# A kernel of four graph-attention layers: score rows spread by DMA through DRAM in place of transposes on TensorE

## Chip, cores and metric

The kernel runs on one core of a Trainium2 chip. The metric is the device time of one execution in microseconds. The engines are named as in the profile: PE (TensorE, with its weight loads PEld), DVE (VectorE), ACT (ScalarE), POOL (GpSimd) and SP (SyncE, which here issues every DMA).

## What is computed

The input is a batch of 128 graphs, each with 128 nodes of 512 features, and an adjacency matrix of 128 x 128 for each. Four layers follow one another. Each takes `h = relu(layernorm(x))` and adds a graph attention over `h` to `x`:

```
layer 0:  scores = leaky(f1[i] + f2[j]), one head, f = h @ (W^T a);  x += elu(softmax(masked scores) @ h)
layer 1:  xl = h @ W1 (4 heads of 256); softmax over the source nodes;  y = elu(att @ xl + b1)
          then xl2 = y @ W2 (one head of 512), attention again;         x += att2 @ xl2 + b2
layer 2:  scores from two dot products of h, one head;                  x += att @ h
layer 3:  xp = h @ W_proj (8 heads of 64); attention;                   x += relu(att @ xp)
```

In every layer a score is the sum of a number of the row's node and a number of the column's node, with a leaky relu of slope 0.2, a mask from the adjacency matrix and a softmax. All data are float32.

## The kernel before

One graph fills the 128 partitions, so a tile is one graph's `x` (128 x 512). Weights are loaded once and prepared in a setup part: the products that give scores are put as extra columns ahead of the weights (`w1x`, `w2x`, `wpx`), so that a projection yields the scores too. A graph is a Python generator, `graph`, which runs `layer0` to `layer3` and yields between stages. A loop lets up to `FLYING` = 7 graphs fly at a time. In each turn it advances each of them by one stage, oldest first, and every `APART` = 11 turns it starts another. So the instructions are written down in an interleaved order, and a planner of the framework then places them on the engines, by that order and by when their inputs are ready, and puts in the semaphores. Each engine works through its own list in order.

The names that matter below:

- `norm_relu` (L178): bn_stats and bn_aggr on DVE (L180, L182), `ve` and `rstd` on POOL (L185, L187), `nmr` on DVE (L190), and `h` on ACT (L192). `h` has three buffers (pool `mid`).
- `dot` (L199): one product of `h` with a vector, on DVE; its results lie in the tile `f0`.
- `transposed` (L217, L219): transposes on PE into a PSUM bank, copied out by ACT.
- `projected` (L284, L293): matmuls with `w1x`, `w2x` or `wpx` on PE, copied to `xl`, `x2` or `x3` by ACT. The first columns of these tiles are the scores.
- `attention`: for each head, a column of scores (one number for each partition) must become a row that stands on all partitions. PE does it with a transpose of the column broadcast over 128 columns (L233). DVE adds the mask and takes the maximum (L240), adds the row's own score (L252 to L259), applies the leaky relu (L262); ACT takes exp with its sum (L266); DVE takes the reciprocal (L275).
- `applied` (L299): the attention matrix is transposed and multiplied with the values.
- layer 1: attention is scaled (L330) and applied (L337), the bias added (L345), and the elu made of L355 (DVE), L357 (exp on ACT) and L359 (DVE), which writes the tile `y` that the matmuls with `w2x` read.
- layer 0 ends with L314 to L319, layer 2 with L378, layer 3 with L393 (PE), L402 and L408 (DVE).
- `loaded` (L415, L419) issues the loads on SP two graphs ahead; the store of a finished graph is L439.

The step that the change replaces is this one:

```
nc.tensor.transpose(
    pb[:, j * P : (j + 1) * P],
    other[:, g + j : g + j + 1].to_broadcast([P, P]),
    ident,
)
```

It is done 15 times for each graph: once in layer 0, four times and once more in layer 1, once in layer 2 and eight times in layer 3.

Of the kernel before, what the change touches and what calls it, by code (L numbers as in the profile page):

```python
# [8 lines left out]
F32 = mybir.dt.float32  # L9
I32 = mybir.dt.int32  # L10
AF = mybir.ActivationFunctionType
ALU = mybir.AluOpType
# [7 lines left out]
FLYING = 7  # L20
# [5 lines left out]
def kernel(  # L26
# [35 lines left out]
    adjp = ctx.enter_context(tc.tile_pool(name="adjp", bufs=3))  # L62
    xpool = ctx.enter_context(tc.tile_pool(name="xpool", bufs=FLYING + AHEAD))
    masks = ctx.enter_context(tc.tile_pool(name="masks", bufs=FLYING))
    big = ctx.enter_context(tc.tile_pool(name="big", bufs=2))
    mid = ctx.enter_context(tc.tile_pool(name="mid", bufs=3))
    small = ctx.enter_context(tc.tile_pool(name="small", bufs=8))
    ps = ctx.enter_context(tc.tile_pool(name="ps", bufs=8, space=PSUM))

    def bank(name):  # L70
        return ps.tile([P, 512], F32, tag="bank", name=name)
# [100 lines left out]


# [49 lines left out]
    def attention(own, other, mask, nh, tag):  # L223
# [4 lines left out]
        for g in range(0, nh, 4):  # L228
            m = min(4, nh - g)
            pb = bank("pb")  # L230
            for j in range(m):

                nc.tensor.transpose(  # L233
                    pb[:, j * P : (j + 1) * P],
                    other[:, g + j : g + j + 1].to_broadcast([P, P]),
                    ident,
                )
            yield
            for j in range(m):
                nc.vector.tensor_tensor_reduce(  # L240
                    out=e[:, g + j, :],
                    in0=pb[:, j * P : (j + 1) * P],
                    in1=mask,
                    scale=1.0,
                    scalar=LOWEST,
                    op0=ALU.add,
                    op1=ALU.max,
                    accum_out=mx[:, g + j : g + j + 1],
                )
# [28 lines left out]
    def projected(lhs, n_k, w, parts, to):  # L278

        width = w.shape[2] // parts  # L280
        for lo in range(0, w.shape[2], width):
            pm = bank("pm")
            for c in range(n_k):
                nc.tensor.matmul(  # L284
                    pm[:, :width],
                    lhsT=lhs[:, c, :],
                    rhs=w[:, c, lo : lo + width],
                    start=(c == 0),
                    stop=(c == n_k - 1),
                )  # L290
                if c % 4 == 3:
                    yield
            nc.scalar.copy(to[:, lo : lo + width], pm[:, :width])  # L293

# [9 lines left out]
    def layer0(xt, mask):  # L304
# [4 lines left out]
        yield  # L309
        e, rz = yield from attention(f[:, 0:1], f[:, 1:2], mask, 1, "e0")  # L310
# [11 lines left out]
    def layer1(xt, mask):  # L322
# [4 lines left out]
        yield from projected(ht, KC, w1x, 3, fx)  # L327
        xl = fx[:, E1:]
        e, rz = yield from attention(fx[:, H1:E1], fx[:, :H1], mask, H1, "e1")
# [32 lines left out]
        yield from projected(y, FC, w2x, 2, gx)  # L362
        yield
        e, rz = yield from attention(gx[:, 1:2], gx[:, 0:1], mask, 1, "e0")
# [3 lines left out]
    def layer2(xt, mask):  # L368
# [4 lines left out]
        yield  # L373
        fb = small.tile([P, 1], F32, tag="fb", name="fb")
        nc.gpsimd.tensor_tensor(fb, f[:, 0:1], b_l2, ALU.add)
        e, rz = yield from attention(fb, f[:, 1:2], mask, 1, "e0")
# [3 lines left out]
    def layer3(xt, mask):  # L380
# [3 lines left out]
        yield from projected(ht, KC, wpx, 2, fx)  # L384
        f, xh = fx[:, :E3], fx[:, E3:]
        yield
        fb = small.tile([P, H3], F32, tag="fb3", name="fb3")
        nc.gpsimd.tensor_tensor(fb, f[:, :H3], b_l3, ALU.add)
        e, rz = yield from attention(fb, f[:, H3:], mask, H3, "e3")
# [32 lines left out]
    def graph(b, xt, a):  # L422
        m0 = masks.tile([P, P], F32, tag="m0", name="m0")
# [6 lines left out]
        yield from layer0(xt, m0)  # L430
# [5 lines left out]
        yield from layer1(xt, m1)  # L436
        yield from layer2(xt, m2)
        yield from layer3(xt, m3)
# [63 lines left out]
```

## Time and profile before

| what | value |
|---|---|
| time, median of 3 runs | 3705.97 us (3705.27 to 3707.51) |
| the profiled execution's own time | 3706.62 us |
| its span, first to last instruction | 3704.8 us |
| PE busy | 3606.2 us, 97% |
| DVE busy | 3075.8 us, 83% |
| ACT busy | 2131.2 us, 58% |
| DMA, mean | 24 GB/s |
| PE clock granted, mean | 0.987 |
| score transposes on PE (L233) | 1920 |

Busy time is the time in which an engine had an instruction in it. Matmuls overlap one another on PE, so a matmul's duration is longer than the time for which it keeps the next one from starting; the distance from start to start is what it costs in a full stretch. The same holds to a lesser degree on DVE and ACT.

### The profile page before, as it was taken

The numbers are of one execution on the slowest core, as the hardware profiler recorded it, in microseconds if no ns is written. First come the engines' busy times: TensorE is split into PE (matmuls) and PEld (weight loads), VectorE is DVE, ScalarE is ACT, GpSimd is POOL, SyncE is SP. The second block draws the span as 40 slices with busy tenths as digits, with TensorE's granted clock in tenths as the row PEclk, the third lists the DMA queues.
The fourth block names the chain that finished last, engine by engine and source line by source line (L and its number), as shares of the span: only waits on it lengthen the run. The fifth ranks groups of instructions, "written<-read, shape, count | busy, mean of one in ns | idle before, by whom it ended". The sixth has DMA issues, their size and how long they took to land.

```text
span 3704.8 us, 60130 instructions
## 1 busy us (share of the span) xinstructions
PE 3606.2 (97%) x19088; PEld 2870.7 (77%) x19088; DVE 3075.8 (83%) x11634; ACT 2131.2 (58%) x6531; POOL 982.2 (27%) x1671
## 2 busy tenths in 40 slices
PE   2999999999999999999999999999999999999997
PEld 1787787788788788788788788788788788778785
DVE  5788888888888888888888888888888888888884
ACT  1455655665565565565665665565565565565563
POOL 1222222222222222222222222232232222222220
PEclk7999999999999999999999999999999999999997
DMA  4000000000000000000000000000000000000000
GB/s 136 4 21 24 21 24 24 21 21 24 21 21 27 21 18 27 21 21 26 21 18 26 21 21 27 21 18 27 21 21 27 20 19 26 21 18 23 16 9 15
DMA packets 60238, 88.54 MB, mean 24 GB/s; under 512 B 7185, under 2 KB 23569, under 8 KB 59921
## 3 DMA queue, kind: packets, MB, share of 16 engines
q1 hardware_dynamic: 59920, 84.70, 6.9%
q8 instruction: 151, 2.47, 0.3%
q14 instruction: 167, 1.36, 0.1%
HBM read 51.13 MB, written 33.55 MB: 23 GB/s over the span
## 4 chain that ended last, share of the span: by engine, by line
PE 96%; DVE 2%; DMA 1%; ACT 1%; POOL 0%; issue 0%; SPq 0%; DVEq 0%; ACTq 0%; POOLq 0%
PE pm L284 60%; PE pt L217 9%; PE pa L299 9%; PE po L337 6%; PE pa L393 6%; PE pb L233 6%; DMA wpx<-in_L_gnn_W_proj_dram 0%; PE ptm L433 0%; ACT e L266 0%; DVE junk L134 0%; DVE st L180 0%; DVE junk L148 0%; DVE e L240 0%; DVE e L262 0%; DVE e L259 0%
## 5 line engine op out<-in xcount | busy, mean ns | idle before, releaser
L266 ACT ACTIVATE e<-e,nm 128x128 f32<-128x128 f32 x1920 | 750.0, 392 | 500.8 <-DVE e L262 494.1
L284 PE MATMUL pm<-w2x,y 128*128 128x257 f32 x4096 | 980.5, 382 | 0.0
L284 PE MATMUL pm<-w1x,ht 128*128 128x344 f32 x3072 | 953.8, 453 | 0.5 <-ACT ht L219 0.5
L284 PEld LDWEIGHTS pm<-w2x,y 128*128 128x128 f32 x4096 | 737.4, 190 | 85.5 <-issue 0.2
L284 PEld LDWEIGHTS pm<-w1x,ht 128*128 128x128 f32 x3072 | 565.1, 191 | 292.7 <-issue 63.1
L319 POOL TENSOR_TENSOR xt<-xt,t 128x512 f32<-128x512 f32 x128 | 163.7, 1279 | 1610.6 <-DVE mv L182 1535.7
L192 ACT ACTIVATE h<-xt,nmr,rstd 128x512 f32<-128x512 f32 x512 | 401.5, 807 | 198.9 <-DVE nmr L190 195.3
L284 PE MATMUL pm<-wpx,ht 128*128 128x264 f32 x2048 | 495.0, 388 | 0.0
L240 DVE CUSTOM_DVE_ANT_0 e<-pb,m 128x128 f32<-128x128 f32 x1920 | 461.6, 280 | 18.2 <-PE pb L233 17.9
L284 PEld LDWEIGHTS pm<-wpx,ht 128*128 128x128 f32 x2048 | 371.9, 192 | 61.9 <-issue 0.2
L217 PE MATMUL pt<-ident,e 128*128 128x128 f32 x1920 | 342.5, 276 | 31.9 <-ACT e L266 21.1
L219 ACT COPY et<-pt 128x128 f32<-128x128 f32 (+1 forms) x768 | 323.4, 421 | 73.3 <-PE pt L217 64.9
L266 ACT ACTIVATION_READ_ACCUMULATOR e<-e,nm 128x1 f32 x1920 | 358.5, 187 | 0.0
L187 POOL TENSOR_TENSOR rstd<-ve,minus_half 128x1 f32<-128x1 f32 x512 | 343.9, 672 | 42.6
L262 DVE SCALAR_TENSOR_TENSOR e<-e 128x128 f32<-128x128 f32 (+2 forms) x640 | 353.8, 553 | 0.0
L180 DVE BATCH_NORM_STATS2 st<-xt 128x6 f32<-128x512 f32 x512 | 342.5, 669 | 3.9 <-POOL xt L319 3.9
L293 ACT COPY x<-pm 128x257 f32<-128x257 f32 (+1 forms) x512 | 184.5, 360 | 269.5 <-PE pm L284 269.2
L293 ACT COPY xl<-pm 128x344 f32<-128x344 f32 x384 | 165.8, 432 | 273.6 <-PE pm L284 273.4
L217 PEld LDWEIGHTS pt<-ident,e 128*128 128x128 f32 x1920 | 243.4, 141 | 68.2 <-ACT e L266 29.2
L359 DVE SCALAR_TENSOR_TENSOR y<-t,y 128x1024 f32<-128x1024 f32 x128 | 156.8, 1225 | 141.3 <-ACT t L357 141.3
L337 PE MATMUL po<-et,xl 128*128 128x128 f32 x2048 | 272.2, 276 | 1.3 <-ACT et L219 1.3
L337 PEld LDWEIGHTS po<-et,xl 128*128 128x128 f32 x2048 | 250.2, 193 | 12.8 <-ACT et L219 2.2
(74 smaller groups left out, 5264.6 us busy)
## 6 DMA issues: line engine op xcount, KB each, us to landing
xt<-in_x_dram SPq DMA_DIRECT2D x128, 256.0 KB, 2.6
out_dram<-xt SPq DMA_DIRECT2D x128, 256.0 KB, 2.0
at<-in_adj_dram SPq DMA_DIRECT2D x32, 256.0 KB, 2.8
w1x<-in_L_gnn_W_dram SPq DMA_DIRECT2D x1, 2048.0 KB, 8.2
w2x<-in_L_gnn_W_dram SPq DMA_DIRECT2D x1, 2048.0 KB, 13.9
wpx<-in_L_gnn_W_proj_dram SPq DMA_DIRECT2D x1, 1024.0 KB, 16.1
w<-in_L_gnn_W_dram SPq DMA_DIRECT2D x1, 1024.0 KB, 9.6
ab<-in_L_gnn_att_src_dram SPq DMA_DIRECT2D x1, 512.0 KB, 4.9
```

What stands on the lines that cost most here:

```text
L180: nc.vector.bn_stats(st6, xt)
L187: nc.gpsimd.tensor_tensor(rstd, ve, minus_half, ALU.pow)
L192: nc.scalar.activation(h, xt, AF.Relu, bias=nmr, scale=rstd)
L217: nc.tensor.transpose(pt[:, j * P : (j + 1) * P], t[:, g + j, :], ident)
L219: nc.scalar.copy(r[:, g : g + m, :].rearrange("p m q -> p (m q)"), pt[:, : m * P])
L240: nc.vector.tensor_tensor_reduce(out=e[:, g + j, :], in0=pb[:, j * P : (j + 1) * P], in1=mask, scale=1.0, scalar=LOWEST, op0=ALU.add, op1= ...
L262: nc.vector.scalar_tensor_tensor(ef, ef, SLOPE, ef, ALU.mult, ALU.max)
L266: nc.scalar.activation(e[:, j, :], e[:, j, :], AF.Exp, bias=nm[:, j : j + 1], accum_out=z[:, j : j + 1],)
L284: nc.tensor.matmul(pm[:, :width], lhsT=lhs[:, c, :], rhs=w[:, c, lo : lo + width], start=(c == 0), stop=(c == n_k - 1),)
L293: nc.scalar.copy(to[:, lo : lo + width], pm[:, :width])
L299: nc.tensor.matmul(pa, lhsT=et[:, 0, :], rhs=values, start=True, stop=True)
L337: nc.tensor.matmul(po[:, (c - g) * P : (c - g + 1) * P], lhsT=xl[:, c * P : (c + 1) * P], rhs=et[:, c * P // F1, :], start=True, stop=True,)
```

## The change

The score rows of most graphs no longer come from PE. `write_rows` issues a DMA on SP which writes the score columns of a tile (1, 4 or 8 for each partition) into a DRAM tile as rows. `read_rows` issues a second DMA, which reads these rows back and spreads them over all 128 partitions of an SBUF tile. `Spread` holds the two together: the read is written down `WRITTEN` = 5 turns after the write, and the first use `READ` = 3 turns after the read. In a projection the write is put right behind the first part, which holds the scores, and the turns of the other parts count. In the first and last `NEAR` = 4 graphs the rows still come from transposes (`far` is false), so that 120 of 128 graphs use the DMAs. `FLYING` goes from 7 to 10, with more buffers for `x` and the masks; the pools are made after the setup part, and a pool `rows` with two buffers for each size and a DRAM pool with four are added.

```diff
-FLYING = 7
+FLYING = 10
+WRITTEN, READ = 5, 3
+NEAR = 4
...
+    dram = ctx.enter_context(tc.tile_pool(name="dram", bufs=4, space=bass.MemoryType.DRAM))
...
+    rows = ctx.enter_context(tc.tile_pool(name="rows", bufs=2))
...
+    def write_rows(cols, n):
+        r = dram.tile([n, P], F32, tag=f"r{n}", name="r")
+        with nc.allow_non_contiguous_dma(reason="a column of scores becomes a row"):
+            nc.sync.dma_start(out=r.rearrange("h p -> p h"), in_=cols)
+        return r
+
+    def read_rows(r, n):
+        t = rows.tile([P, n, P], F32, tag=f"rb{n}", name="rb")
+        nc.sync.dma_start(
+            out=t.rearrange("p h q -> p (h q)"),
+            in_=r.rearrange("h q -> (h q)").partition_broadcast(P),
+        )
+        return [t[:, j, :] for j in range(n)]
+
+    class Spread:
+        def __init__(self, cols, n, far):
+            self.cols, self.n, self.far = cols, n, far
+            self.turns = 0
+            self.r = write_rows(cols, n) if far else None
+
+        def turn(self):
+            self.turns += 1
+            if self.far and self.turns == WRITTEN:
+                self.rows = read_rows(self.r, self.n)
+
+        def rest(self):
+            if self.far:
+                while self.turns < WRITTEN + READ:
+                    yield
+                    self.turn()
+                return self.rows
...
-    def attention(own, other, mask, nh, tag):
+    def attention(own, rb, mask, nh, tag):
...
-                nc.tensor.transpose(
-                    pb[:, j * P : (j + 1) * P],
-                    other[:, g + j : g + j + 1].to_broadcast([P, P]),
-                    ident,
-                )
-            yield
...
+        for j in range(nh):
+            nc.vector.tensor_tensor_reduce(
+                out=e[:, j, :],
+                in0=rb[j],
...
-    def projected(lhs, n_k, w, parts, to):
+    def projected(lhs, n_k, w, parts, to, cols, far):
...
                 if c % 4 == 3:
                     yield
+                    if sp:
+                        sp.turn()
             nc.scalar.copy(to[:, lo : lo + width], pm[:, :width])
+            if lo == 0:
+                sp = Spread(cols, cols.shape[1], far)
+        yield
+        sp.turn()
+        return (yield from sp.rest())
...
     def graph(b, xt, a):
+        far = NEAR <= b < B - NEAR
```

In the texts below x2, x3 and xl are the score columns of the projections with `w2x`, `wpx` and `w1x`, and f0 and f2 those of the dots in layers 0 and 2.

## The prediction

> **What bounds the kernel now.** I read the busy shares first, then a steady stretch, then the chain of waits.
>
> ```profile
> PE 3606.2 (97%) x19088; PEld 2870.7 (77%) x19088; DVE 3075.8 (83%) x11634; ACT 2131.2 (58%) x6531; POOL 982.2 (27%) x1671
> ```
> ```profile
> 1800.00:2100.00 300.00, 300.00 (x1608) 239.91 (x1607) 255.10 (x967) 177.57 (x544) 80.33 (x136) 1.00 0.07 23
> ```
> ```profile
> PE 96%; DVE 2%; DMA 1%; ACT 1%; POOL 0%; issue 0%; SPq 0%; DVEq 0%; ACTq 0%; POOLq 0%
> ```
>
> In 300 us of steady running PE (second number) is never idle, at full clock (1.00); the chain that ended last runs through PE. The timeline of PE gives the price of each piece by its starts:
>
> ```profile
> 1800.25 0.60 PE L217 MATMUL pt<-ident,h 128*128 128x128 f32 x4
> ...
> 1806.38 0.27 PE L233 MATMUL pb<-ident,f 128*128 128x128 f32 x1
> 1806.49 1.95 PE L284 MATMUL pm<-wpx,ht 128*128 128x264 f32 x8
> ...
> 1828.11 0.60 PE L217 MATMUL pt<-ident,h 128*128 128x128 f32 x4
> ```
>
> The same transposes return after 1828.11 - 1800.25 = 27.86 us: one graph. A score transpose (L233) lasts 0.27 but holds PE 0.11. Times below are such start-to-start spacings.
>
> **What the Trainium skill says.** "DMA: Bandwidth & Descriptors", Two DMAs through the same engine are not ordered: a DMA that reads what another wrote must wait, on its issuing engine, for the writer's semaphore. The trace agrees: each x load waits behind the store of its buffer.
>
> ```profile
> 1835.00 0.34 SPq L439 DMA_DIRECT2D out_dram<-xt  x1
> 1837.07 0.33 SPq L419 DMA_DIRECT2D xt<-in_x_dram  x1
> ```
>
> The same page, Rules for kernel authors: a non-contiguous last dimension becomes one descriptor per element. No steady DMA here is of that kind. "TensorE: Matmul & The Clock Gate", Part 1: after some 3.4 us idle PE's clock falls to half. The trace shows a low clock (0.60) where PE is busy 19 of 50 us:
>
> ```profile
> 50.00:100.00 50.00, 18.85 (x56) 11.78 (x57) 31.12 (x111) 12.23 (x29) 15.17 (x23) 0.60 0.02 5
> ```
>
> **What is removed.** 15 score transposes for each of 120 graphs: 15 x 0.11 = 1.63 us, so PE needs 27.86 - 1.63 = 26.2 us a graph. If PE stayed full that would be all: -196 us.
>
> **What is added.** Per graph five writes and five reads on SP, at 0.34 us of issue (rows above): 3.4 us, with 0.96 MB read. As bandwidth that is nothing (the DMA share is 0.07). What counts is the order. The planner, which places every instruction as soon as its inputs are ready, does not keep the five and three turns. In the built order of the instructions SP's period is: x2 write, f0 write, their reads, xl write, x3 write, their reads, f2 write, its read, store, load. Each pair of reads stands right behind its writes, so SP waits there for the landing, with all later writes queued behind it; the x load queued last is not missed, since it comes two graphs (55 us) ahead of its use. DVE uses the rows at once as well: `e0` on x2's row directly follows the dots that give f0, and the eight `e3` on x3's row directly follow `e1`. While DVE waits there, these are queued behind: the end of layer 0, layer 2's dots, `y` of layer 1 and the end of layer 3. This order repeats exactly for 112 of 128 graphs. So that the spread does not keep the distance that the code asks for is no rival but my starting point.
>
> **The loop that this closes** runs from the end of the elu's `y` instruction (L359), which PE's w2x matmuls await, to the end of the next graph's. Every engine works in order, so each step below waits for the one above. Lines are those of before; spacings are from the DVE, ACT, PE and POOL timelines of before.
> - DVE to h: variance to `nmr` through POOL took 1829.47 to 1830.96, 1.49; twice, with `nmr` 0.08 and L330 0.61 between: 3.67. Then small ones and masks of layer 2's e0: 0.75. Its leaky relu to the ACT start 0.32, exp 0.40. ACT has that exp ahead of layer 3's h (0.81): 5.95, say 6.0.
> - PE behind that h: five transposes 0.55, one w2x matmul 0.435, a transpose 0.11, four w2x 1.74, four w1x 2.32, four transposes 0.44, four wpx 1.78: 7.37.
> - ACT copies x3: 0.27 until it starts, 0.36: 14.0 in all.
> - SP writes x3's 8 columns (w), then reads them as rows (r).
> - DVE: seven `e3` 1.47, L316 0.33, `e3` 0.21, L317 0.65, two dots 1.22, bn_stats delayed by POOL's add of t0 to 4.72; neg, add, small ones, relu to 7.2; two L345, L402, L408 to 10.2; L355, mask, xt, small ones, bn_stats 2.3, which cover ACT's exp; L359 1.15: 13.65.
>
> Sum: 14.0 + 13.65 = 27.65 + w + r. Without any DMA time it is already the present period.
>
> **The unknown DMA times.** w: not below the store's landing, 2.0. x3 is 1024 elements of 4 bytes, 64 per DMA engine; queue q1's packets took on average 6.9% of 16 x 3704.8 / 59,920 = 68 ns, 4.4 us for 64. Doubling it for a partial write gives at most 2 + 2 x 4.35 = 10.7, a floor 2.0; I take 5.2. r: an x load lands in 2.6; 256 KB more at the slope to w1x (2048 KB in 8.2) is 0.8: 3.4, ends 2.6 and 4.
>
> ```profile
> xt<-in_x_dram SPq DMA_DIRECT2D x128, 256.0 KB, 2.6
> out_dram<-xt SPq DMA_DIRECT2D x128, 256.0 KB, 2.0
> ```
>
> So 27.65 + 8.6 = 36.3. PE is not late in this: its last po matmuls, 14 us of work after wpx, end near 28, while DVE's second L345 starts at 14.0 + 8.6 + 8.5 = 31. PE then idles 10 us a graph, most of it in one piece before w2x, so its clock drops: between 0 (slack before h) and 2 us; I take 0.5: **36.8**, or 8.94 more a graph. Floor: with short DMAs x2's row still holds DVE. Its copy stands on ACT behind the h at 5.95, two `ht` copies, layer 0's h and an `et` copy, 8.4; w 2.0 and r 2.3 make 12.7; the reciprocal behind both `e0` needs exps that stand behind x3's copy, 14.5; L366, bn_stats and POOL's 1.49 again make 17.3, `e1` 2.4: 19.7, and 13.65 more is 33.3. Ceiling: 27.65 + 10.7 + 4 + 2 = 44.3.
>
> The other edits: the row buffers (two of each size) and DRAM tiles (four) are free again before they are wanted, since each row is used at once: 0. Ten graphs in flight cost nothing (x and mask buffers only), but `h` keeps three buffers and lives longer, part of why the planner found little else to put in the gaps; taken as inside the loop. DVE reading rows from SBUF instead of PSUM: L257 (SBUF) 280 ns and L240 (PSUM) 280 ns, so 0; ends -0.5 and +0.5 us a graph. Near graphs keep transposes: 0. Moving pools: 0, set before the loop. Filling with longer graphs and draining: within +-40 us.
>
> **Sum.** Against the profiled execution's own 3706.6 (span 3704.8; 0.6 above the median 3705.97): 116 graphs (112, and half of the mixed eight) x 8.94 = 1037, so 4744, say **4740**.
>
> **Rivals.**
> - PE stays the bound: DMA hidden behind five and three turns. For it: a turn is 27.86 / 11 = 2.5 us, so the code asks for 13 us between write and read and 8 to the use, more than any landing above; DVE needs but 255.1/300 of its time. Against: the built order. Time 3706 - 196 = 3510. It decides only if w + r falls below 27.86 - 27.65 = 0.2 us, or if most of my in-order edges (exp ahead of h on ACT, `e3` ahead of the rest on DVE) were absent. Chance 0.06.
> - Short DMA, so that the path through x2's row and `e1` sets the period, 33.3: 116 x 5.4 = 631, 4340. For it: stores land in 2.0. Against: 1024 separate elements. 0.27.
> - Element writes as slow as the doubled packet, or a cold PE: 40 to 44: 5120 to 5600. 0.2.
> - My middle, a period of 34.5 to 39.5 (4480 to 5060): 0.46. No change at all: 0.01.
>
> A measurement of this kernel tells about 0.2% from none. The changes that are slower hold 0.93, the faster 0.06. The range leaves out the faster case and the far ends of the two others: 4280 to 5200.
>
> **What would show it.** Right: PE busy near 70% in steady stretches, its longest wait for the w2x matmuls on the elu's `y` (DVE), and for layer 3's h on ACT; DVE waiting for DMA at the `e3` line 3 us or more in each graph; SP waiting at the read line for the write; a steady period of 33 to 40 us; a clock below 1.00. Each step has its row: landing of the x3 write and of the 512 KB read, POOL's 1.49, PE's 7.37. Wrong: PE at 97% with a period of 26.2; or reads that DVE never waits for; or x3 rows landing within 4 us yet a period over 36, which would put the loss on another edge.

## The result, and the profile after

The changed kernel takes 6548.6 us (median of 4 runs, 6534.4 to 6554.5), against 3705.9 before (4 runs): a ratio of 1.766, 95% interval 1.763 to 1.770. The profiled execution took 6554.5 us, its span 6552.7. The forecast was slower, 4740 us with a range of 4280 to 5200: right in sign, far off in size.

The busy shares (busy time of each engine, its share of the span, number of instructions), then a steady stretch in the middle of the run (length, then busy time of each engine with its instructions, granted clock of PE, DMA share, GB/s), then the chain that ended last, by engine and by line (`r` is the DRAM tile with the rows, `rb` the rows in SBUF, so `r<-f` is a write of f0 or f2 and `r<-x` one of x2 or x3):

```profile
PE 4223.2 (64%) x17288; PEld 3155.1 (48%) x17288; DVE 3140.8 (48%) x11634; ACT 2065.3 (32%) x6531; POOL 1105.7 (17%) x1671
```
```profile
3000.00:3500.00 500.00, 322.80 (x1313) 243.96 (x1314) 242.52 (x893) 160.50 (x510) 88.02 (x130) 0.76 0.15 32
```
```profile
DMA 64%; DVE 19%; ACT 6%; PE 6%; issue 2%; SPq 1%; POOL 1%; ACTq 0%; DVEq 0%; POOLq 0%
DMA r<-f 20%; DMA r<-xl 20%; DMA rb<-r 16%; DMA r<-x 7%; DVE junk L204 6%; PE pm L328 3%; DVE e L282 2%; ACT e L308 2%; DVE e L304 2%; ACT h L197 2%; PE pt L222 2%; DVE e L301 2%; DVE t L368 1%; SPq L237 1%; ACT t L365 1%
```

No engine is full any more. PE, which was never idle in the steady stretch before, has work in 323 of 500 us and runs at 0.76 of its clock. The chain has changed hands: 64% of it are transfers, above all the writes of f0 or f2, the write of xl, and the reads of rows.

The issues and their median time from issue to landing, the moment from which a waiting engine can go on:

```profile
rb<-r SPq DMA_DIRECT2D x120, 512.0 KB, 4.3
...
out_dram<-xt SPq DMA_DIRECT2D x128, 256.0 KB, 5.3
rb<-r SPq DMA_DIRECT2D x120, 256.0 KB, 4.7
...
r<-f SPq DMA_DIRECT2D x240, 0.5 KB, 7.8
```

A write of 128 numbers, 0.5 KB, takes 7.8 us, longer than the read of 512 KB, and the store of x, the same instruction as before, takes 5.3 in place of 2.0. SP's timeline shows what that does to one period (start and duration of each issue; SP waits in between):

```profile
3018.30 0.32 SPq L232 DMA_DIRECT2D r<-f  x1
3026.00 0.32 SPq L237 DMA_DIRECT2D rb<-r  x1
...
3036.22 0.32 SPq L232 DMA_DIRECT2D r<-x  x1
3036.66 1.17 SPq L232 DMA_DIRECT2D r<-f  x1
3044.29 0.87 SPq L237 DMA_DIRECT2D rb<-r  x2
3045.21 0.43 SPq L232 DMA_DIRECT2D r<-xl  x1
3045.69 0.50 SPq L232 DMA_DIRECT2D r<-x  x1
3056.28 1.49 SPq L237 DMA_DIRECT2D rb<-r  x2
```

The writes are f2's at 3018.30, then x2's and f0's, then xl's and x3's. The two reads at 3044.29, 7.6 us after f0's issue, wait for the landings of x2 and f0, which were issued 0.4 us apart and take 8.1 each. Only then does SP get to the writes of xl and x3. The first read behind these waits until 3056.28 for xl's, 11.1 us after its issue and 10.6 after x3's; the second, x3's, is issued 1.2 us later. These two landings stand one behind the other in each period. DVE waits for the rows (us in total, number of waits, longest; then single lines of its timeline, with the wait ahead of each in brackets):

```profile
DVE e L282 <- DMA rb<-r: 2560.9, 434, 17.3
```
```profile
3025.86 1.21 DVE L410 SCALAR_TENSOR_TENSOR y<-t,y 128x1024 f32<-128x1024 f32 x1
3031.10 0.29 DVE L282 CUSTOM_DVE_ANT_0 e<-rb,m 128x128 f32<-128x128 f32 x1 [1.09 <-DMA rb<-r]
3048.72 0.29 DVE L282 CUSTOM_DVE_ANT_0 e<-rb,m 128x128 f32<-128x128 f32 x1 [12.09 <-DMA rb<-r]
3061.00 0.29 DVE L282 CUSTOM_DVE_ANT_0 e<-rb,m 128x128 f32<-128x128 f32 x1 [3.92 <-DMA rb<-r]
3076.16 1.21 DVE L410 SCALAR_TENSOR_TENSOR y<-t,y 128x1024 f32<-128x1024 f32 x1
```

That is 2561 us in 434 waits. One period in full, read off the timelines of SP and DVE:

| step | us |
|---|---|
| end of `y` (L410) at 3027.06 to the end of f0's dots and its write on SP at 3036.66 | 9.6 |
| from f0's write until the first of the two reads, at 3044.29, when x2's has landed | 7.6 |
| two reads and xl's write issued, until x3's write | 1.4 |
| from x3's write until xl's, issued 0.5 earlier, has landed | 10.6 |
| read of xl's rows, until `e1` starts at 3061.00 | 4.7 |
| `e1`, `e3` and on to the end of the next `y` at 3077.36 | 16.4 |
| sum, and distance of the two `y` | 50.3 |

The first step hides a third landing. f2's write, issued at 3018.30, is awaited until 3026.00, and the read of its row takes 5.1 more. Behind it stand layer 2's `e0` at 3031.10, its exp and two `h` on ACT, and then f0's dots. In this period the chain that ended last runs there and not through `y`; in the next it runs through `y` and PE. From the start of `e1` to f0's write it is 26.0 us by f2's row (3010.70 to 3036.66) and 26.3 by `y` (3061.00 to 3087.28), so the two ways are level. Over the whole span `r<-f` and `r<-x` hold 27% of the chain, about 1770 us. If all of that were single columns, at 7.8 us each, it would be some 230 landings in 120 periods (an estimate): beside xl's, mostly two.

### The profile page after: what moved, and what is told of

Same layout as the page of the kernel before. It is cut to its first block, busy times and chain, and to the rows that moved or that the text cites. A ratio compares the mean times of both kernels' runs of the same rounds, so it can differ in the third digit from the quotient of the medians.

```text
span 6552.7 us, 58807 instructions
## 1 busy us (share of the span) xinstructions
PE 4223.2 (64%) x17288; PEld 3155.1 (48%) x17288; DVE 3140.8 (48%) x11634; ACT 2065.3 (32%) x6531; POOL 1105.7 (17%) x1671
## 4 chain that ended last, share of the span: by engine, by line
DMA 64%; DVE 19%; ACT 6%; PE 6%; issue 2%; SPq 1%; POOL 1%; ACTq 0%; DVEq 0%; POOLq 0%
DMA r<-f 20%; DMA r<-xl 20%; DMA rb<-r 16%; DMA r<-x 7%; DVE junk L204 6%; PE pm L328 3%; DVE e L282 2%; ACT e L308 2%; DVE e L304 2%; ACT h L197 2%; PE pt L222 2%; DVE e L301 2%; DVE t L368 1%; SPq L237 1%; ACT t L365 1%
## 5 line engine op out<-in xcount | busy, mean ns | idle before, releaser
L282 DVE CUSTOM_DVE_ANT_0 e<-rb,m 128x128 f32<-128x128 f32 x1800 | 439.4, 289 | 2596.1 <-DMA rb<-r 2560.9
L328 PE MATMUL pm<-w2x,y 128*128 128x257 f32 x4096 | 1234.4, 451 | 391.4 <-DVE y L410 391.4
L328 PEld LDWEIGHTS pm<-w2x,y 128*128 128x128 f32 x4096 | 896.0, 230 | 765.8 <-DVE y L410 562.0
L442 PE MATMUL pa<-x,et 128*128 128x64 f32 x2048 | 413.8, 372 | 1020.3 <-ACT et L224 1020.3
L442 PEld LDWEIGHTS pa<-x,et 128*128 128x128 f32 x2048 | 390.4, 285 | 1039.6 <-ACT et L224 1039.4
L350 PE MATMUL pa<-h,et 128*128 128x512 f32 x512 | 374.1, 823 | 377.8 <-ACT et L224 371.5
L388 PE MATMUL po<-et,xl 128*128 128x128 f32 x2048 | 423.5, 375 | 295.5 <-ACT et L224 295.2
L190 POOL TENSOR_SCALAR ve<-mv 128x1 f32<-128x1 f32 x512 | 223.3, 436 | 1990.3 <-DVE mv L187 1605.9
L388 PEld LDWEIGHTS po<-et,xl 128*128 128x128 f32 x2048 | 384.9, 280 | 360.3 <-ACT et L224 359.7
L370 POOL TENSOR_TENSOR xt<-xt,t 128x512 f32<-128x512 f32 x128 | 207.9, 1624 | 1431.8 <-DVE t L368 1396.9
```

The source lines that it names most:

```text
L282: nc.vector.tensor_tensor_reduce(out=e[:, j, :], in0=rb[j], in1=mask, scale=1.0, scalar=LOWEST, op0=ALU.add, op1=ALU.max, accum_out=mx[:, ...
L328: nc.tensor.matmul(pm[:, :width], lhsT=lhs[:, c, :], rhs=w[:, c, lo : lo + width], start=(c == 0), stop=(c == n_k - 1),)
L350: nc.tensor.matmul(pa, lhsT=et[:, 0, :], rhs=values, start=True, stop=True)
L388: nc.tensor.matmul(po[:, (c - g) * P : (c - g + 1) * P], lhsT=xl[:, c * P : (c + 1) * P], rhs=et[:, c * P // F1, :], start=True, stop=True,)
L442: nc.tensor.matmul(pa[:, k * K3 : (k + 1) * K3], lhsT=et[:, k, :], rhs=xh[:, k * K3 : (k + 1) * K3], start=True, stop=True,)
```

## Experiments

The theory at the start (A): transfers of elements of 4 B are what is slow, and two of them stand in series in the loop. Its rivals: the read back of rows is slow; DVE or the planner's order is slow by itself; SP is held by its own waits, whatever the rows are used for. The edits shown are shortened, and the comments in them are added here.

**A probe of the transfers.** Into the kernel before went a chain of unused DMAs beside every fourth graph, each of which waits for the one ahead:

```diff
+        nc.sync.dma_start(out=p[0:1, :].rearrange("h p -> p h"), in_=b1[:, 0:1])
+        back(1, "qa")       # broadcast of 1 row
+        nc.sync.dma_start(out=p[0:8, :].rearrange("h p -> p h"), in_=b1[:, 0:8])
+        back(8, "qb")       # broadcast of 8 rows
+        nc.sync.dma_start(out=p[:, :], in_=w_src[:, 0:P])
+        back(1, "qc")
+        nc.sync.dma_start(out=p[0:1, :], in_=w_dst[0:1, 0:P])
+        back(1, "qd")
```

> The kernel before, with a chain of eight extra DMAs on SP beside every fourth graph, whose data nobody uses; each waits for the one ahead, so each lands alone: a column of 128 elements written as a row, its 64 KB broadcast back, 8 columns written (1024 elements), their 512 KB broadcast, a 128 x 512 B write, a broadcast, one 512 B row from one partition, a broadcast. Theory A (four-byte elements are what lands late): 7 to 8 us for the column, 10 to 13 for the 8 columns, 2 to 3 for the wide write and for the row. Rival B (a DRAM tile is slow to write, or the queue was crowded in the changed kernel): the four writes land within 2 us of each other, at 7 or more if the tile is slow, at 2 to 3 if it was crowding. Both: broadcasts 2.5 to 5, the time within 1% of 3706.

3709.2 us, one run. One such chain in SP's timeline; the distance to the next line is the landing:

```profile
1088.28 0.43 SPq L254 DMA_DIRECT2D pr<-b  x1
1095.62 0.33 SPq L245 DMA_DIRECT2D qa<-pr  x1
1100.22 0.37 SPq L257 DMA_DIRECT2D pr<-b  x1
1111.23 0.32 SPq L245 DMA_DIRECT2D qb<-pr  x1
1114.95 0.32 SPq L259 DMA_DIRECT2D pr<-w_src  x1
1116.91 0.32 SPq L245 DMA_DIRECT2D qc<-pr  x1
1119.76 0.24 SPq L261 DMA_DIRECT2D pr<-w_dst  x1
```

A run is a stretch of bytes without a gap. 128 elements into one row 7.3, 1024 into eight rows 11.0; 128 runs of 512 B only 2.0. The medians of all 28 chains are 7.8, 10.5 and 1.6. The broadcast of one row took 4.6 behind the elements and 2.85 behind the runs (medians 4.6 and 2.8), although the write had landed before it was issued. So the writes are slow also where nothing else of the change is there, and eight times the elements cost but a third to a half more.

**The transfers alone.** The kernel before, with its transposes, and all ten DMAs of the change beside them; nobody reads the rows.

```diff
+    def unused(cols, n, far):
+        if far:
+            read_rows(write_rows(cols, n), n)
```

> The kernel before with its transposes, which also issues all ten spreading DMAs of each of the 120 graphs; nobody reads the rows, so no engine but SP ever waits for them. If it is the waits of DVE for rows alone that cost, 3700 to 3730. If DMA traffic slows the engines, the same order with longer instructions, over 3800. If SP's own holds (each read stands behind its write in SP's order) are a limit by themselves, the sum of the holds decides: about 9 us for the three single columns together, 12 for x3, 12 for xl, 2 to 5 for the store ahead of the load, some 37 us for a graph against 27.9, so loads of x come late and the time is 4500 to 4900.

5162.0 us in a single run, more than the 4500 to 4900 expected. The waits of SP, and then those of ACT, show two holders that have nothing to do with rows being used:

```profile
SPq L190 <- DMA r<-x: 2109.7, 219, 14.9
```
```profile
ACT x L316 <- DMA r<-x: 1405.9, 155, 16.1
```

SP stands before reads until the writes have landed, so later writes start late; and the copy into x2 or x3 on ACT may not overwrite a tile whose write is still to come or under way. PE's next transposes wait for that copy. A late write therefore costs even if its row is never wanted.

**Short writes, same order.** Each write becomes n runs of 512 B from n partitions; everything else, the built order too, stays. The rows then hold other numbers than the scores, so this kernel serves for its time alone.

```diff
-            nc.sync.dma_start(out=r.rearrange("h p -> p h"), in_=cols)
+        nc.sync.dma_start(out=r, in_=cols[0:n, 0:P])      # cols is now a tile of 128 columns or more
```

> The changed kernel, the same instructions in the same order on each engine; only the write takes n runs of 512 B from n partitions in place of 128 n elements of 4 B (so the rows hold other numbers than the scores). Theory A: writes land in 2 to 3 us, and the loop of 50.6 us a graph loses 7.7 - 2.2 at f0 and 11 - 2.2 at xl and x3: 36 us a graph, 4500 to 4800. Rival B (DRAM tile or queue, whatever the size of the runs): writes at 7 or more still, 6300 to 6600.

4503.7 us, ratio 1.216 (1.212 to 1.219): as theory A had it. Of the 2843 us lost, 2045 go with the form of the writes; 798 stay.

**One half each.** The same edit for the single columns only (`if n == 1`), and for the four and eight columns only.

> The changed kernel, in which only the writes of a single column (x2, f0, f2) are one run of 512 B from one partition instead of 128 elements of 4 B; the writes of four and eight columns stay by elements. The order of the instructions is the same on every engine. The rows of those three layers hold other numbers than the scores. Theory A, two landings in series per graph (the f0 write, then the xl and x3 writes that stand behind it on SP): the f0 landing falls from 7.7 to about 2, so the period falls by 5.7 us and some 1.5 us of the reads that follow it, from 50.6 to 43.4 - 44.9: 6549 - 112 x 5.7 to 7.2 = 5740 to 5910, taken 5800. Rival, one landing in the loop, the long one of x3 (as the forecast had it): the single columns are off the path and the time stays above 6400.

> The other half: only the writes of four and eight columns (xl, x3) are 4 and 8 runs of 512 B; the single columns stay by elements. Same order of the instructions; the rows of layers 1 and 3 hold other numbers than the scores. Theory A: the second landing falls from 11 - 12.8 to about 2, 9 to 10.8 us of 50.6: 6549 - 112 x 9 to 10.8 = 5340 to 5540, taken 5440. If the landings are in series, the two savings add up to that of the kernel in which all writes are short (6549 - 4504 = 2045); if they lie side by side, they add up to clearly less, each being hidden by the other. Rival: the f0 write hides what is won, time above 6000.

5611.0 and 5588.9 us: 938 and 960 less than the changed kernel, together 1897 of the 2045 that both bring. The distance from store to store on SP, averaged over some twenty graphs, goes from 51.2 us to 43.3 and 43.1, and to 34.4 with both. If the landings lay side by side, taking one away would bring little; they add up, so they stand in series. Each size was missed, the first too small, the second too large: the single columns bring 7.9 us a period where 5.7 was expected for f0's landing alone, which fits f2's landing in the chain.

**SP in the written turns.** Each spread DMA is held behind the one written before it on SP.

```diff
-            nc.sync.dma_start(out=r.rearrange("h p -> p h"), in_=cols)
+            tc.keep_in_program_order(nc.sync.dma_start(...))     # the read likewise
```

> The changed kernel with the spreading DMAs held on SP in the order in which they are written down (five writes, then the reads five turns later); the other engines are ordered by the planner as before. If it is the order on SP (reads right behind their writes) that exposes the slow landings, the writes overlap and are hidden, and the chain through y of layer 1 is left: 32 to 35 us a graph, 4150 to 4500. If the DMAs are too slow to be hidden in any order, over 5500.

5471.4 us, ratio 1.477 (1.472 to 1.481), a miss. The five turns on SP are there now, and still the reads come late:

```profile
3036.74 0.42 SPq L232 DMA_DIRECT2D r<-f  x1
3037.26 12.74 SPq L237 DMA_DIRECT2D rb<-r  x5
```
```profile
SPq L237 <- DMA rb<-r: 1126.8, 114, 12.9
```

Five reads stand right behind f2's write, and SP needs 12.7 us for them. Four are issued within 2 us; the fifth, f2's, waits for an earlier read of a single row to land, since there are two buffers for these. The first of the reads, issued at 3037.26 right behind f2's element write, is for a row written long before, and still DVE gets it only at 3049.35, 12.1 us later.

**All rows a full period later.** To give the rows real time, each read stands 8 or 9 turns behind its write and each use 5 or 6 turns later, so that every attention comes exactly 11 turns after its old place. DVE's first use of rows and the spread DMAs keep the written order; all 128 graphs spread by DMA.

```diff
+FLYING = 12
...
+            if self.far and self.turns == self.when[0]:
+                self.rows = read_rows(self.r, self.n)
...
+        rb = yield from Spread(f[:, 1:2], 1, far, (8, 5)).rest()      # (9, 5), (9, 6), (8, 5), (9, 5) for the others
```

> All five spreads by DMA with element writes as in the change, but each row is read 8 or 9 turns after its write and used 5 or 6 turns later, 13 to 15 turns in place of the change's 8, so that every attention stands one full period of 11 turns after its place in the kernel before; FLYING 12, five buffers for h, four for the single rows, masks to match; all graphs alike; the DMAs on SP and the first use of a row on VectorE keep the written order. Theory A, the slow transfers cost only because nothing stands between write and read in the built order: now 20 us lie between write and read and 12 us to the use, no wait of VectorE for rows is left to speak of, and TensorE bounds it as in the kernel before, with 15 transposes less: 128 x 26.2 + 140 + about 100 for the longer filling and emptying: 3600, range 3450 to 3750. Theory B, SP's own in-order waits and the queueing of reads behind element writes keep the loop closed whatever the distance: 4200 to 5200, as the kernel with unused rows (5162) would have it.

5740.6 us, ratio 1.548 (1.546 to 1.551). Distance alone does not hide the transfers; here is SP in that kernel:

```profile
3042.12 0.38 SPq L231 DMA_DIRECT2D r<-f  x1
3042.60 0.38 SPq L490 DMA_DIRECT2D out_dram<-xt  x1
3043.03 0.42 SPq L236 DMA_DIRECT2D rb<-r  x1
3043.57 0.38 SPq L231 DMA_DIRECT2D r<-f  x1
3052.55 0.33 SPq L469 DMA_DIRECT2D xt<-in_x_dram  x1
```

The load at 3052.55 wants the buffer of the store at 3042.60, which stood behind the element writes of x2 and f0: 10 us for a transfer that took 2.0 before (the median), and 1001 us in 114 such waits. I took this wait, and reads that stand right behind x3's write, for the whole of it, and cleared both:

**The same, sorted.** Loads one graph ahead with the same buffers, reads up to three turns earlier so that none follows an element write that it doesn't need, loads and stores in the written order too.

```diff
-AHEAD = 2
+AHEAD = 1
-        rb = yield from projected(ht, KC, w1x, 3, fx, fx[:, :H1], far, (9, 5))
+        rb = yield from projected(ht, KC, w1x, 3, fx, fx[:, :H1], far, (7, 7))    # (5, 8), (8, 7), (8, 5), (8, 6) for the others
```

> The kernel with all five spreads one period later (5741), with three things changed on SP: an x is loaded one graph ahead and not two, with the same 14 buffers, so that a load no longer waits for the store of the graph that has just ended; the reads are moved by up to three turns, so that no read of rows is issued right behind an element write that it doesn't need (the row of layer 1 now ahead of x3's write); loads and stores keep the written order with the rest. Each use stays where it was. Theory, what held the 5741 is SP: a load held it for 9 us a graph until the store behind the element writes had landed, and reads that stood behind x3's 1024 elements landed 12.7 us after their issue and came late: with both gone VectorE waits for rows no more and TensorE bounds the kernel: 128 x 26.2 + 140 + about 100: 3600, range 3500 to 3850. Rival, the 1920 elements per graph keep the rings so busy that reads and stores land late wherever they stand: 4300 to 5500, with VectorE still waiting on rows.

5836.2 us, ratio 1.573 (1.568 to 1.578). That theory fell. The rival's range was missed as well, but its picture is in the trace: DVE waits 2161.6 us for rows. A read of 256 KB issued at 3001.95, right behind f2's write and ahead of x3's, was awaited until 3018.18, 16.2 us, and an adjacency load behind xl's write took 11.4 us, with DVE waiting both times:

```profile
3018.18 0.29 DVE L281 CUSTOM_DVE_ANT_0 e<-rb,m 128x128 f32<-128x128 f32 x1 [12.21 <-DMA rb<-r]
```
```profile
3034.23 0.23 DVE L475 TENSOR_SCALAR m<-at 128x128 f32<-128x128 int32 x1 [9.70 <-DMA at<-in_adj_dram]
```

**The same, sorted, with short writes.** The number and the order of DMAs on SP stay.

> The kernel with all spreads a period later and SP's order sorted (5836), in which only the writes change: n runs of 512 B from n partitions in place of 128 n elements of 4 B; the rows hold other numbers than the scores. The number and order of the DMAs on SP stay, those of the other engines too but for a few places at the start. Theory 1, element writes into one row hold whatever stands in the same rings (loads, stores and reads landed 10 to 16 us after their issue there): with them gone the rows come in time and TensorE is the bound with 15 transposes less: 3550 to 3850. Theory 2, SP's written order closes the loop by itself, since a write that waits for its scores holds the reads behind it: 4500 to 5600, VectorE still waiting for rows.

3557.9 us, ratio 0.960 (0.959 to 0.962), as theory 1 had it. So SP's order does not close a loop of its own; the element writes hold the transfers that stand near them, in what way is open. The two causes in one table (us). Within a row only the writes differ; between the rows there are also the flying graphs, buffers and held order named above:

| | element writes | short writes |
|---|---|---|
| rows used as the planner built the change | 6549 | 4504 |
| rows used a period later, sorted | 5836 | 3558 |

Each cure alone leaves the kernel slower than before; only both bring PE back to its bound.

**What makes an element write slow.** A second probe beside the kernel before, each write followed by a read of 32 B that waits for it:

```diff
+            nc.sync.dma_start(out=p[0:1, :].rearrange("h p -> p h"), in_=b1[:, 0:1])           # (a), L251
+            one(0)                                              # the read; it follows each of the others too
+            nc.sync.dma_start(out=p[:, 0:1], in_=b1[:, 0:1])                                   # (b), L254
+            nc.sync.dma_start(out=p[:, 0:8], in_=b1[:, 0:8])                                   # (c), L256
+            nc.sync.dma_start(out=p[0:1, 0:16].rearrange("h p -> p h"), in_=b1[0:16, 0:1])     # (d), L258
+            nc.sync.dma_start(out=p[0:16, 0:1], in_=b1[0:16, 0:1])                             # (e), L260
+        nc.sync.dma_start(out=p[:, :], in_=w_src[:, 0:P])                                      # (f), L262
```

> The kernel before, with a chain of unused writes to a DRAM tile beside every fourth graph, each followed by a read of 32 B from its first row into one partition, which waits for the landing: (a) 128 elements of 4 B into one row of 512 B, (b) 128 elements, each into a row of its own, 512 B apart, (c) 128 runs of 32 B, one per row, (d) 16 elements into one row, (e) 16 elements, each into a row of its own, (f) 128 rows of 512 B. Theory 1, small writes into the same 64 or 512 B hinder each other: (a) 7.3, (b) and (c) 2 to 3, (d) 3 to 7, (e) 2, (f) 2.0. Theory 2, every element of 4 B has its price wherever it goes, or any write under a certain size has one fixed price: (b) and (e) as long as (a) and (d), 6.5 to 7.3; (c) then tells 32 B from 4 B. The time of the whole kernel stays within 0.3 per cent of that before.

3709.1 us, one run.

```profile
1200.72 0.43 SPq L251 DMA_DIRECT2D pr<-b  x1
1208.50 0.24 SPq L245 DMA_DIRECT2D qa<-pr  x1
1211.58 0.32 SPq L254 DMA_DIRECT2D pr<-b  x1
1212.99 0.23 SPq L245 DMA_DIRECT2D qa<-pr  x1
1214.16 0.32 SPq L256 DMA_DIRECT2D pr<-b  x1
1215.56 0.24 SPq L245 DMA_DIRECT2D qa<-pr  x1
1216.69 0.32 SPq L258 DMA_DIRECT2D pr<-b  x1
1218.00 0.22 SPq L245 DMA_DIRECT2D qa<-pr  x1
1220.60 0.30 SPq L260 DMA_DIRECT2D pr<-b  x1
1221.91 0.22 SPq L245 DMA_DIRECT2D qa<-pr  x1
```

(a) 7.8 us; (b) 1.4, the same 128 elements of 4 B, each into its own row; (c) 1.4; (d) 1.3, sixteen into one row; (e) 1.3 as well. So neither the size nor the number of the elements makes the 7.8: it is many of them into one row of 512 B. The reads of 32 B say the same. Behind (a) the read takes 3.1 and behind (d) 2.6, although these writes had landed, but 1.1 to 1.2 behind (b) and (c). So sixteen elements into one row are not free either; their price comes with the read. (a) stands right behind an x load, which lands in 2.6 and so cannot account for the 6.4 between (a) and (b). The changed kernel itself was then run with its elements apart, each in 64 B of its own, so that eight share 512 B:

```diff
-            nc.sync.dma_start(out=r.rearrange("h p -> p h"), in_=cols)
+            nc.sync.dma_start(out=r.rearrange("p (h s) -> p h s", s=16)[:, :, 0], in_=cols)
```

> The changed kernel, with as many elements of 4 B in every write as before, 128, 512 and 1024, but each element goes into 64 B of its own, in a DRAM tile that was filled ahead of the graphs; the reads take as many contiguous bytes from it, so the rows hold other numbers than the scores. The order of the instructions is that of the changed kernel. Theory 1, what is slow is many elements into the same 512 B: the writes land in 1.4 to 2 us and the kernel comes to where short writes bring it (4504): 4400 to 4800. Theory 2, every element of 4 B has its price: 6200 to 6700. Between: part is the number of elements, above all in the writes of 1024.

4822.0 us, ratio 1.301 (1.299 to 1.303), a little above the range of theory 1.

```profile
r<-f SPq DMA_DIRECT2D x240, 0.5 KB, 1.4
```

With the order and the number of elements unchanged, f0's and f2's writes land in 1.4 in place of 7.8, xl's in 3.2 in place of 11.7, x3's in 3.8 in place of 12.8, and the store of x in 2.0 again (medians). 1727 of the 2045 us are thus due to elements packed into the same rows, the reads of such rows included; 318 are left for their number. Eight elements in 512 B are fast here, so the line lies somewhere between that and 128; no run says where, nor whether 512 B or a smaller stretch counts.

**Layer 3 alone.** The kernel before, with only the eight rows of layer 3 by DMA, a period later; then with the held order on DVE for that layer only; then the same lateness with transposes and no DMA.

```diff
-        yield from layer0(xt, m0, far)
+        yield from layer0(xt, m0, False)      # layers 1 and 2 likewise
```

> The kernel before, in which only the eight scores of layer 3 go by DMA (element writes), read 9 turns after the write and used 5 turns later, one period later than before; FLYING 8. The other layers keep their transposes. TensorE loses 8 transposes of 0.11 us per graph. If the transfer is hidden: 3706 - 120 x 0.87 = 3600, plus up to 40 for one graph more in flight: 3600 to 3650. If the copy into x3 or SP's order still waits for the write of 1024 elements (11 us) each graph: 3750 to 4300.

> The kernel with layer 3 alone by DMA one period later (3783), in which only the first use of layer 3's rows is held to the written order on VectorE, and the attentions of the other layers are free again for the planner. There VectorE waited for rows in 6 places only (29.5 us in all), so the transfer was hidden, and yet TensorE waited for the dots of f0 and f2 1.3 us a graph (163.9 in all, line 269). Theory, the held order on VectorE made that wait: with it gone TensorE is the bound with 8 transposes less, 27.0 a graph: 3706 - 120 x 0.87 = 3600, plus up to 40 for one graph more in flight: 3600 to 3650. Rival, with its rows in SBUF and one graph more in flight VectorE, now the end of the chain at 62%, is the bound whatever the order: 3740 to 3800.

> The kernel with layer 3 alone a period later (3785), in which the eight rows of layer 3 come from eight transposes again, made a turn before their use; no spread DMA is left, and FLYING 8, the lateness of layer 3 and the held first use on VectorE stay. Theory 1, the lateness and the order that the planner builds with it cost about 3785 - 3600: the time is 3785 + 128 x 0.87 = 3850 to 3900. Theory 2, the transfers cost it (contention of the rings or the memory): 3706 to 3750.

3783.3 us (ratio 1.021, 1.019 to 1.023), 3785.3 (1.022, 1.021 to 1.023) and 3856.7 (1.041, 1.039 to 1.042). The first hope failed and so did the theory of the held order. The second time lies in its rival's range, but DVE is busy in 252 of 300 us there, so that it is the bound is not shown. The third kernel splits the sum: lateness alone, with the order that the planner builds around it, costs 151 us; against that, taking eight transposes a graph to the DMA brings 71. In the first of these, DVE waited for rows in six places (29.5 us in all). One element write a graph, with a period to land, is hidden.

**A version that keeps the scores right and the writes short.** One transpose turns the n columns of a spread into n rows on n partitions; ACT copies them to SBUF, and the DMA writes n runs of 512 B. Five transposes a graph in place of fifteen.

```diff
+                nc.tensor.transpose(self.pb[: self.n, :P], self.cols, ident)
...
+                row = small.tile([self.n, P], F32, tag=f"row{self.n}", name="row", bufs=2)
+                nc.scalar.copy(row, self.pb[: self.n, :P])
+                self.r = write_rows(row, self.n)
```

> The kernel with all spreads a period later and SP's order sorted (5836), with the true scores in short writes: a transpose on TensorE turns the n columns of a spread at once into n rows on n partitions, ScalarE copies them to SBUF, and the DMA writes n runs of 512 B to DRAM a turn later than the element writes stood; the broadcast reads and their uses stay. Five transposes per graph in place of the fifteen of the kernel before. From the kernel with short writes of other numbers (3558): 128 x 5 x 0.11 = 70 more on TensorE, 3628, if the five copies on ScalarE, about 0.3 us each, stay beside other work; range 3580 to 3690, below the kernel before. Rival: the copies and the turn lost between scores and write make rows late again, or the planner's order turns worse, as it did for layer 3 alone: 3720 to 4000.

4102.0 us, ratio 1.107 (1.106 to 1.109): missed. PE works in order and stood at these transposes:

```profile
PE pb L249 <- ACT x L344: 278.3, 136, 3.8
PE pb L249 <- DVE nmr L194: 95.1, 117, 1.6
```

So the transpose was put two turns, and one turn, after the scores, with the copy and the write a turn later.

> The kernel with one transpose per spread (4102), its transpose made two turns after the scores and not at once, the copy and the write a turn after that; reads and uses stay. Theory, TensorE, in order, stood at the transpose until ScalarE had copied the scores, 3.7 us a graph, and the rest of the loss follows from that stand: two turns later the scores are there, and the kernel comes to 3558 + 128 x 5 x 0.11 = 3628; range 3580 to 3690, 1 to 3 per cent ahead of the kernel before. Rival, the five copies on ScalarE and the banks they hold set the time: above 3800.

> The same with the transpose one turn after the scores, copy and write a turn after that. Theory: part of the wait on TensorE may be left, 3600 to 3850; not below the kernel with two turns by more than 20. Rival (copies): above 3800 as well.

3719.5 us (ratio 1.004, 1.002 to 1.005) and 3599.2 us (0.971, 0.970 to 0.973). Both expectations were missed: two turns came out too slow, and one turn is 120 us faster than two, where no more than 20 was expected. One turn is enough, and this version beats the kernel before by 2.9%. Its steady stretch and chain:

```profile
1800.00:2100.00 300.00, 300.00 (x1569) 235.13 (x1568) 267.98 (x1012) 190.66 (x628) 93.12 (x148) 1.00 0.18 59
```
```profile
PE 93%; DVE 3%; ACT 1%; POOL 1%; issue 0%; DMA 0%; POOLq 0%; ACTq 0%; DVEq 0%
```

PE is never idle again, at full clock, with ten transposes a graph less: 107 us, 0.083 for each if all of it is put down to them. Why two turns are worse than one is open: in that kernel PE waits 82 us for ACT's copies `ht` and is busy 292 of 300 us. Each lateness gave another order of the planner, and the order, not the lateness, seems to decide; that was not tried further.

## Why the prediction was right or wrong

- **The spread does not keep its distance: right.** The built order stood in the trace line by line. What it costs was not priced apart: 798 us of the 2843 stay with short writes, and go, with another 148, once the rows come a period later and SP's order is sorted.
- **PE needs 26.2 us a graph: right.** In the kernel with short writes a period later, where no transpose and next to no wait was left (PE busy in 298.7 of 300 us), stores on SP came 26.4 us apart. As the bound it would have given 3510; that kernel took 3558.
- **The loop, 27.65 + w + r with x3's write as its one landing: here it failed.** Term by term, with the period above:

| term | taken | measured |
|---|---|---|
| from `y` to x3's write | 14.0 | 18.6 |
| w, landing awaited behind x3's write | 5.2 (2.0 to 10.7) | 10.6 |
| r, read of rows | 3.4 (2.6 to 4) | 4.7 |
| DVE to the next `y` | 13.65 | 16.4 |
| cold PE | 0.5 | within the others |
| sum | 36.8 | 50.3 |

  - The first term has the path wrong. x3's scores were taken to be written when ACT had copied them. But on SP this write stands behind the reads of x2 and f0, and these behind the landings of x2's and f0's writes, which lie side by side: 9.6 + 7.6 + 1.4. The prediction named this order itself ("with all later writes queued behind it") and then put no landing of a single column into its loop; only its floor has one, at 2.0, where 7.6 stood in the path. At 2.0 the first term would be 13.0, less than the 14.0 of the copy. f2's landing, in the 9.6, was not in it either.
  - The second has the size wrong, and the write: SP waits there for xl's (11.1), not x3's. x3's rows are taken at 3063.38 without a wait. The ceiling of 10.7, a doubled packet for each of 64 elements on a DMA engine, met the number by luck: elements apart land far sooner (x3's in 3.8).
  - The third: right behind element writes a read takes longer, 4.6 in place of 2.85 for one row in the probe.
  - The fourth: DVE waits for xl's rows, so `e1` (3061.00 to 3063.38, 2.4 us) stands in the path ahead of `e3`; without it 14.0 is left.

  The four miss 4.6, 5.4, 1.3 and 2.7 us a period. The mean period on SP is 51.2; with the prediction's 116 graphs that makes 3707 + 116 x (51.2 - 27.86) = 6414, and some 135 us of the 6549 were not traced further.
- **One descriptor per element: the Trainium skill's warning was right, its weight was mine to find.** The rule of "DMA: Bandwidth & Descriptors" (Rules for kernel authors) that a non-contiguous last dimension becomes one descriptor per element agrees with the trace: packets under 512 B went from 7185 to 256,784. But their number accounts for 318 us only, by the kernel with elements apart, which has as many of them (258,001). The same page (Queues, rings and completion order) says that on each DMA engine descriptors are consumed in ring order, which agrees with reads, loads and stores landing 10 to 16 us after their issue behind element writes. That the rings (the queues of descriptors) as such are what holds them is argued; that the element writes do it is shown by the short ones.
- **A read waits on the issuing engine for the write: right.** The load behind a store that the prediction showed only overwrites what the store reads. The case itself is in the changed kernel: SP waits 3248 us in all at the reads of rows for the writes of them.
- **The x load is not missed: wrong in part.** Hardly any engine waits for x, but the store that the load waits for holds SP: 532 us in 116 waits at the load.
- **PE idles and grows cold: right, and more.** 64% busy where 70 was forecast, the clock at 0.763. What the clock alone cost was not separated; PE has 6% of the chain that ended last. The longest waits of PE, taken at its weight loads, were at layer 3's values (1039 us, for ACT's copy of the transposed attention), not at `y` (562).
- **The rivals.** Slow elements (5120 to 5600, chance 0.2) had about the right landing and was still 950 us short: against its ceiling of 44.3 us a graph, the period above has 4.6 more for the second landing and 2.7 for `e1`, with 0.7 for the read, and the 2.0 for a cold PE did not come on top. PE as the bound failed for the reason given, the built order; and the run a period later shows that order alone would not have saved it. The range was too narrow because all its slow cases shared the single landing.

## What to carry to other kernels

Follow every wait of the issuing queue in its order before pricing a loop: a read that waits for a write holds all later writes on that queue, and their landings add. Then read in the chain which of them is awaited last. Turn a column into a row on chip and write runs of 512 B: here many elements into one row cost some 7 to 11 us and delayed the transfers around them too. That alone is not enough: a distance written in turns is worth what the built order leaves of it, and short writes in the planner's order were still 22% slower than no DMA. A new producer in front of an in-order engine can stop it; here one turn of lead was enough.

## What the runs showed of the hardware

- 128 elements of 4 B into one row of 512 B landed in 7.3 and 7.8 us in the chains shown (medians of the two probes 7.8 and 7.9); the same into 128 rows in 1.4; 128 runs of 32 B in 1.4; sixteen elements into one row in 1.3; 128 runs of 512 B in 2.0 (median 1.6). 1024 elements into eight rows took 11.0 (median 10.5).
- A read of 32 B from a row that had just been written by elements took 2.8 (after 128) and 2.6 (after sixteen) in place of 1.1 (medians of 28 chains); the broadcast of one such row 4.6 in place of 2.8.
- With such writes on the same queue the store of x took 5.3 (median) in place of 2.0, and an adjacency load 11.4 (one, a period later and sorted) in place of 2.8 (median before). With as many elements set 64 B apart the store took 2.0.
- Five transposes of n columns a graph, with ACT's copies (0.25 us for 8 x 128), cost 3599 - 3558 = 41 us over 640 of them, 0.065 us each: the difference of two kernels, whose orders are not quite the same.
